# The second layer norm's mean by an extra projection column and its squares on ScalarE, in a hybrid attention kernel

## The chip, the cores and the metric

The kernel runs on one core of one Trainium2 chip. The metric is the device time of one execution in microseconds (us). The engines are called PE (TensorE), DVE (VectorE), ACT (ScalarE), POOL (GpSimd) and SP (SyncE); ACT, SP and POOL also issue DMA transfers, each from its own queue. L978 is line 978 of the kernel before; the lines of the kernel after are higher by one to thirty.

## The reference, cut to what matters

Input is an image of 256 channels and 64 x 64 pixels, in float32. Layer 0 is a windowed linear attention on group-normalised channels and is added to the image. Layer 1 takes the 4096 pixels as tokens of 256 channels:

```python
t = t + attention(layer_norm(t))          # 8 heads of 32, softmax over 4096 keys, w_out, b_out
t = t + experts(layer_norm(t))            # the second norm: of what the line above gave
# layer_norm: (v - mean(v)) / sqrt(var(v) + 1e-5), over the 256 channels of a token
# experts: norm once more, two of 8 experts for each token by softmax of xt @ Wr,
#          gelu(xe @ W1) @ W2, weighted sum
```

The change is about the second norm: each token's mean and variance over its channels after the attention's output has been added.

## The kernel before, in words

All activations stay in on-chip memory. The residual stream is the tile `t`, 32 token tiles of 128 tokens by 256 channels and 8 more columns: the tokens' scores for the 8 experts before normalisation. The weight `wo` (attention's output projection) has the same 8 more columns, made on PE from `w_out` and `Wr`, so one projection gives both a tile's attention output and its part of the scores.

The stages are layer 0 (to about 1037 us), the first norm and the projections to queries, keys and values (to 1155), the attention (1155 to 2412), routing (to some 2460), 36 expert slots, and the output.

The attention goes over eight chunks of 512 queries (`qc`), two groups of four heads (`g`), and 32 tiles of 128 keys (`i`). A step `i` is:
- PE: four products of keys and queries, one a head, into two pairs of banks of `ps_two` (L969; three pairs are there),
- ACT: two exponentials of 1024 columns into one buffer of `pe` (L978; four buffers),
- DVE: the buffer is added to `total`, for the denominators (L984), except at steps 0, 15 and 31 (step 1 adds the two first),
- PE, one step later: the products with the values, accumulated in `ps_acc` (L938), and at steps 15 and 31 also the products with ones, into the denominator bank `ps_den`, which has one buffer.

Work for the end of a group is spread over the next group's steps by a list of chains: `take` (copy of `ps_acc`, L1001), `pack` (the products of `total` with ones, the copy of `ps_den` to `rec`, L1022, and two transfers that pack the denominators densely), three empty steps, `turn` (the reciprocal, L1030, and five transfers that spread it again), three empty steps, `spread` (the multiplication, L1007).

When chunk `qc - 1` is done for both head groups, its four token tiles are projected. This is put into the steps of group `g = 1` of chunk `qc`:

```python
if qc and g == KC - 1 and i in range(5, NT // 2, 3):
    done.append(NB * (qc - 1) + len(done) % NB)
    project(den_bank(), done[-1])
```

so at steps 5, 8, 11 and 14, into the denominator bank that is not in use there. `project` is two matmuls (L919), an addition to `t` on DVE (L922) and `norm2.stats`, two DVE instructions (L740 and L741). The last four tiles are projected behind the loop.

The order of instructions on an engine isn't that of the code alone: a scheduler places each instruction when the kernel is built, by its own estimate of when its data are there. Engines then run their own instructions in that fixed order and wait for each other by semaphores.

Behind the attention, the second norm is finished (L745 to L749), the normalised tokens `z` are made by ACT (L1195) and stored, and the experts' scores are corrected by mean and deviation (L1209 to L1212). Small weights for the experts come by ACT's queue (L1172), are transposed by PE (L1174) and copied by DVE (L1175).

Of the kernel before, what the change touches and what calls it, by code (L numbers as in the profile page):

```python
# [34 lines left out]
NT = N // P  # L35
# [5 lines left out]
NB = IMG // BH  # L41
# [5 lines left out]
NE = 8  # L47
# [64 lines left out]
def tile_conv_attn_hybrid(ctx: ExitStack, tc: tile.TileContext, a: dict, out: bass.AP):  # L112
    nc = tc.nc

    const = ctx.enter_context(tc.tile_pool(name="const", bufs=1))
    keep = ctx.enter_context(tc.tile_pool(name="keep", bufs=1))
# [15 lines left out]

    t = keep.tile([P, NT, C + NE], F32, name="t")

    wr_sum = keep.tile([P, NE], F32, name="wr_sum")
    act = keep.tile([P, KC, N], F32, name="act")

    def tok(i):  # L140
        return slice(P * i, P * (i + 1))
# [44 lines left out]
    with ExitStack() as phase:  # L186
        wts = phase.enter_context(tc.tile_pool(name="c_wts", bufs=1))
# [22 lines left out]
        with (  # L210
# [34 lines left out]
            for b in range(NB):  # L245
# [6 lines left out]
                for ix in range(0, NCH, 2):  # L252
                    tp = bank("tp")
# [6 lines left out]
                    to, tp = tb[:, b, ix : ix + 2, :C], tp.rearrange("p (i c) -> p i c", c=C)  # L260
# [24 lines left out]
            rstd = rstd_of(small, var_ps[:, :KC], KC, 1e-5)  # L285
            for k in range(KC):
# [5 lines left out]
                    op0=ALU.subtract,  # L292
                    op1=ALU.mult,
# [461 lines left out]
            nc.tensor.transpose(tp[:, tok(k)], src[:, tok(k)], ident)  # L755
        nc.scalar.copy(dst, tp[:, :C].rearrange("p (k n) -> p k n", k=KC))

    norm2 = Norm(keep, "ln2")


    with ExitStack() as phase:
        pool = lambda name, bufs: phase.enter_context(tc.tile_pool(name=name, bufs=bufs))
        big = pool("a_big", 1)
        wts = pool("a_wts", 1)
        small = pool("a_small", 1)

        wo = wts.tile([P, KC, C + NE], F32, name="wo")
        nc.scalar.dma_start(wo[:, :, :C], a["L1_attn_w_out"].rearrange("(k p) o -> p k o", p=P))


# [6 lines left out]
        with (  # L777
# [23 lines left out]
            for n, by in enumerate((lambda k: ones[:, :1], lambda k: bqk[:, 4 + k : 5 + k])):  # L801
                for k in range(KC):
# [4 lines left out]
                        start=k == 0,  # L807
                        stop=k == KC - 1,
# [5 lines left out]
            for j in range(KC):  # L814
                tp = ps.tile([P, CH], F32, tag="mm", name="ps_mm")
# [3 lines left out]
            tp = ps.tile([P, CH], F32, tag="mm", name="ps_mm")  # L819
            for k in range(KC):  # L820
                for j in range(KC):
# [4 lines left out]
                        start=j == 0,  # L826
                        stop=j == KC - 1,
                    )
            nc.vector.tensor_copy(wo[:, :, C:], tp[:, : KC * NE].rearrange("p (k e) -> p k e", e=NE))

            norm = Norm(small, "ln1")

# [6 lines left out]
            for c in range(NCH):  # L839
                if c + 1 < NCH:  # L840
                    begin(c + 1)
                norm.end(NB * c, NB * (c + 1))
                for i in range(NB * c, NB * (c + 1)):
                    hn = work.tile([P, C], F32, name="hn")
                    nc.vector.tensor_scalar(
                        hn,
                        t[:, i, :C],
                        norm.mean[:, i : i + 1],
                        norm.rstd[:, i : i + 1],
                        op0=ALU.subtract,  # L850
                        op1=ALU.mult,
                    )
                    to_channels(hn, act[:, :, tok(i)], ps)

                    nc.gpsimd.tensor_add(t[:, i, :C], t[:, i, :C], bo)
                for s in range(2):
                    for g in range(KC):
                        m = KC * s + g
                        pr = ps.tile([P, CH], F32, tag="mm", name="ps_mm")
                        for k in range(KC):  # L860
                            nc.tensor.matmul(
                                pr, wqkv[:, k, tok(m)], act[:, k, chunk(c)], start=k == 0, stop=k == KC - 1
                            )
                        to = qk[:, s, g, chunk(c)]
                        nc.vector.tensor_scalar_add(to, pr, bqk[:, m : m + 1])
                        nc.vector.tensor_reduce(
                            peak[:, s, g, c : c + 1], to, AX.X, ALU.max, apply_absolute_value=True
                        )
                for i in range(NB * c, NB * (c + 1)):
                    pv = ps.tile([P, CH], F32, tag="mm", name="ps_mm")  # L870
                    for k in range(KC):
                        nc.tensor.matmul(
                            pv[:, : C + NE],
                            act[:, k, tok(i)],
                            wqkv[:, k, 2 * C :],
                            start=k == 0,
                            stop=k == KC - 1,
                        )
                    nc.vector.tensor_add(v[:, i, :], pv[:, :C], bv)
                    nc.scalar.copy(t[:, i, C:], pv[:, C : C + NE])  # L880


            on_experts = lambda z: z.unsqueeze(2).to_broadcast([P, NT, NE])
            on_tiles = lambda z: z.unsqueeze(1).to_broadcast([P, NT, NE])
            std = win.tile([P, NT], F32, name="std")
            nc.vector.tensor_scalar_add(std, norm.var, 1e-5)
            nc.vector.tensor_mul(std, std, norm.rstd)
            nc.vector.tensor_mul(t[:, :, C:], t[:, :, C:], on_experts(std))
            shift = win.tile([P, NT, NE], F32, name="shift")
            nc.vector.tensor_mul(shift, on_experts(norm.mean), on_tiles(wr_sum))  # L890
            nc.vector.tensor_add(shift, shift, on_tiles(bo_wr))
            nc.vector.tensor_add(t[:, :, C:], t[:, :, C:], shift)

# [11 lines left out]
            tp = ps.tile([P, CH], F32, tag="mm", name="ps_mm")  # L905
# [9 lines left out]
        attnT = act  # L915

        def project(pr, i):
            for k in range(KC):
                nc.tensor.matmul(  # L919
                    pr[:, : C + NE], attnT[:, k, tok(i)], wo[:, k, :], start=k == 0, stop=k == KC - 1  # L920
                )
            nc.vector.tensor_add(t[:, i, :], pr[:, : C + NE], t[:, i, :])  # L922
            norm2.stats(i)

        with tc.If(tame > 0) as branch:  # L925
            with (
# [5 lines left out]
                def two_banks():  # L932
                    return ps.tile([P, 2, CH], F32, tag="two", name="ps_two", bufs=3)
# [16 lines left out]
                by_ones = (NT // 2 - 1, NT - 1)  # L950
# [3 lines left out]
                done = []  # L954

                def den_bank():
                    return ps.tile([P, CH], F32, tag="den", name="ps_den")

                for qc in range(NCH):
                    for g in range(KC):  # L960
# [4 lines left out]
                        for i in range(NT):  # L965
                            sc = [two_banks() for _ in range(2)]
                            for hd in range(4):
# [5 lines left out]
                                    start=True,  # L973
                                    stop=True,
# [21 lines left out]
                            if i == NT - 1:  # L996
                                to = attnT[:, g, chunk(qc)]
# [41 lines left out]
                                def spread(times=times, held=held):  # L1039
                                    times(held.pop())  # L1040

                                wait = [lambda: None] * 3
                                if qc == NCH - 1 and g == KC - 1:
                                    stages = [take, divide]
                                else:
# [1 line left out]
                            behind(*stages)  # L1047


                            if qc and g == KC - 1 and i in range(5, NT // 2, 3):  # L1050
                                done.append(NB * (qc - 1) + len(done) % NB)
                                project(den_bank(), done[-1])
                flush()
                for i in range(len(done), NT):
                    project(two_banks()[:, 0, :], i)
        with branch.Else():


            with (
# [8 lines left out]
                for hd in range(2 * 4):  # L1068
                    g, hs = hd // 4, slice(D * (hd % 4), D * (hd % 4 + 1))
                    nc.vector.tensor_copy(ka[:D, :], qk[hs, 1, g, :])  # L1070
                    for qc in range(NCH):
# [16 lines left out]
                        for i in range(NT):  # L1088
# [4 lines left out]
                            for j, lhsT in enumerate((v[:, i, D * hd : D * (hd + 1)], ones)):  # L1093
# [4 lines left out]
                                    start=i == 0,  # L1098
# [5 lines left out]
                        nc.vector.tensor_mul(attnT[hs, g, chunk(qc)], acc[:D, :], rec)  # L1104
                for i in range(NT):
                    project(ps.tile([P, CH], F32, tag="sc", name="ps_sc"), i)

    with ExitStack() as phase:
# [17 lines left out]
        def one(name):  # L1129
            return small.tile([P, NT], F32, name=name)  # L1130
# [30 lines left out]
        with ExitStack() as routing:  # L1161
# [18 lines left out]

            norm = norm2
            norm.begin(0, NT)
            norm.end(0, NT)
            again = one("again")
            nc.vector.tensor_mul(again, norm.var, norm.rstd)
            nc.vector.tensor_mul(again, again, norm.rstd)
            again = rstd_of(small, again, NT, 1e-5)
            nc.vector.tensor_mul(again, again, norm.rstd)  # L1190
            less = one("less")
            nc.vector.scalar_tensor_tensor(less, norm.mean, -1.0, again, op0=ALU.mult, op1=ALU.mult)
            z = big.tile([P, NT, C], F32, name="z")
            for i in range(NT):
                nc.scalar.activation(  # L1195
                    z[:, i, :], t[:, i, :C], AF.Identity, scale=again[:, i : i + 1], bias=less[:, i : i + 1]
                )
# [11 lines left out]
            nc.vector.tensor_mul(logit, on_experts(norm.mean), on_tiles(wr_sum))  # L1209
            nc.vector.tensor_sub(logit, t[:, :, C:], logit)  # L1210
            nc.vector.tensor_mul(logit, logit, on_experts(norm.rstd))
            nc.vector.tensor_add(logit, logit, on_tiles(br))  # L1212

            rank = on_tiles(cst["rank"])
# [258 lines left out]
```

## Time and profile before

| | |
|---|---|
| three runs | 3022.8, 3024.1 and 3033.7 us, median 3024.1 |
| the profiled execution | 3024.6 us; its span, from first to last instruction, 3022.8 us |
| attention loop, PE / DVE / ACT busy (1158 to 2400, 1242 us) | 1196.4 / 1114.3 / 993.2 us |
| busy over the span: PE, DVE, ACT, POOL | 94%, 68%, 50%, 25% |
| mean granted clock of PE | 0.97 |
| DVE, L740: 64 statistics of 256 columns, mean | 417 ns |
| DVE, L741: 64 aggregations, mean | 174 ns |
| DVE, L922: 28 additions in the loop, mean | 425 ns |

The page gives groups of instructions: line, engine, operation, output and inputs, how many, then busy time in us and the mean of one in ns, then the engine's idle time just before them and what ended most of it. A line of waits gives the waiting instruction, the one it waited for, the total in us, how often, and the longest. A line of the timeline gives start, duration, engine, line and operation, how many in a row, and in brackets the idle time before it. A matmul's end is modelled, and four matmuls of 32 rows run beside each other, so their durations don't add up.

### The profile page before, as it was taken

Reading aid. Unit: us, or ns where it says so; the run is one execution under the profiler, and the core shown is the slowest. Engines: PE = TensorE matmul, PEld = TensorE weight load, DVE = VectorE, ACT = ScalarE, POOL = GpSimd, SP = SyncE. Lnnn points to the kernel's source line nnn. Section 1 sums busy time; section 2 is a strip of 40 time slices with the busy share of each in tenths; the row PEclk is TensorE's granted clock in tenths of the full one; section 3 lists DMA queues with packets and bytes.
Section 4 is the critical chain, followed back from the end, with each engine's and each line's share of the span. In section 5 each row is a group of like instructions: output and inputs, shape, how many; then the busy total and the mean of one; then the engine's idle time right before and its main releaser. Section 6 shows DMA issues by size and latency. Waiting matters only on the chain.

```text
span 3022.8 us, 62433 instructions
## 1 busy us (share of the span) xinstructions
PE 2835.8 (94%) x26550; PEld 1366.5 (45%) x26550; DVE 2067.7 (68%) x2510; ACT 1510.2 (50%) x2079; POOL 742.6 (25%) x832
## 2 busy tenths in 40 slices
PE   6899999989999899999999999999999879999996
PEld 5456443736543453222222222222222248888884
DVE  5776768577677787998888988898889841111113
ACT  2242323133233216887878787878778642222222
POOL 4085857128577420000000000000000012222220
PEclk9999999999999999999999999999999969999997
DMA  2000000000000000000000000000000055566565
GB/s 84 6 2 4 2 3 2 7 1 3 3 2 3 18 1 1 5 5 5 5 5 5 5 5 5 5 5 5 5 5 5 6 186 194 187 202 190 195 194 197
DMA packets 92627, 133.24 MB, mean 44 GB/s; under 512 B 16914, under 2 KB 73976, under 8 KB 92340
## 3 DMA queue, kind: packets, MB, share of 16 engines
q1 hardware_dynamic: 78008, 101.12, 10.2%
q0 software_dynamic: 6912, 18.88, 2.2%
q10 hardware_dynamic: 7420, 9.15, 0.9%
q8 instruction: 212, 3.47, 0.5%
q14 instruction: 75, 0.61, 0.1%
HBM read 111.00 MB, written 18.12 MB: 43 GB/s over the span
## 4 chain that ended last, share of the span: by engine, by line
PE 32%; DVE 23%; DMA 2%; ACT 2%; issue 1%; SPq 0%; DVEq 0%; POOL 0%; ACTq 0%; POOLq 0%
DVE total L984 22%; PE ps_yp L1394 8%; PE ps_hp L1387 8%; PE ps_two L969 7%; PE ps_acc L938 6%; PE ps_den L938 1%; ACT pe L978 1%; DMA y<-yrows 1%; PE ps_acc L1311 1%; ACT z L1195 1%; PE ps_tp L1362 1%; DMA rec<-recs 0%; DMA recs<-some 0%; DMA some<-dens 0%; DMA dens<-rec 0%
## 5 line engine op out<-in xcount | busy, mean ns | idle before, releaser
L978 ACT ACTIVATE pe<-ps_two 128x1024 f32<-128x1024 f32 x1024 | 992.9, 1022 | 246.9 <-PE ps_two L969 219.9
L984 DVE TENSOR_TENSOR total<-total,pe 128x2048 f32<-128x2048 f32 x448 | 1024.9, 2288 | 56.3 <-ACT pe L978 16.1
L969 PE MATMUL ps_two<-qk 32*128 32x512 f32 x4096 | 639.9, 644 | 3.6 <-POOLq L925 1.9
L938 PE MATMUL ps_acc<-pe,v 128*32 128x512 f32 x4096 | 551.4, 610 | 27.0 <-DVE act L1001 26.8
L533 ACT COPY sm<-ps_sc 128x384 f32<-128x384 f32 (+4 forms) x486 | 232.6, 513 | 462.9 <-PE ps_sc L657 272.7
L537 POOL TENSOR_TENSOR sm<-sm,mask 128x192 f32<-128x192 f32 (+3 forms) x460 | 380.2, 863 | 227.7 <-ACT sm L533 227.2
L969 PEld LDWEIGHTS ps_two<-qk 32*128 32x128 f32 x4096 | 211.1, 184 | 425.8 <-PE ps_two L969 250.7
L537 DVE TENSOR_TENSOR sm<-ps_sc,mask 128x384 f32<-128x384 f32 (+3 forms) x708 | 323.8, 518 | 91.0 <-PE ps_sc L657 89.9
L1388 ACT ACTIVATE hid<-ps_hp,cols 128x256 f32<-128x256 f32 x288 | 136.5, 474 | 382.3 <-PE ps_hp L1387 382.3
L1237 POOL MEMSET on<- 128x256 f32 x1 | 0.3, 312 | 1256.1 <-PE ps_den L938 1256.1
L938 PEld LDWEIGHTS ps_acc<-pe,v 128*32 128x32 f32 x4096 | 81.0, 108 | 420.7 <-issue 379.7
L1387 PE MATMUL ps_hp<-xe,w 128*128 128x256 f32 x1152 | 256.3, 381 | 0.0
L1394 PE MATMUL ps_yp<-w,hid 128*128 128x256 f32 x1152 | 254.6, 379 | 0.0
L657 PE MATMUL ps_sc<-qk 32*128 32x192 f32 (+3 forms) x2688 | 243.8, 444 | 4.6 <-DVE sm L537 2.9
L1394 PEld LDWEIGHTS ps_yp<-w,hid 128*128 128x128 f32 x1152 | 216.4, 190 | 28.1
L1387 PEld LDWEIGHTS ps_hp<-xe,w 128*128 128x128 f32 x1152 | 208.2, 190 | 41.9 <-ACT hid L1388 5.2
L673 PE MATMUL ps_acc<-sm,v 128*32 128x192 f32 (+3 forms) x2688 | 216.1, 422 | 0.8 <-POOL sm L537 0.8
L1366 DVE TENSOR_SCALAR xe<-ps_tp,cols 128x256 f32<-128x256 f32 x72 | 35.8, 540 | 248.5 <-PE ps_tp L1362 228.7
L537 POOL TENSOR_TENSOR sm<-sm,ycut 128x384 f32<-128x384 f32 (+4 forms) x150 | 150.9, 1026 | 145.6 <-ACT sm L533 145.4
L657 PEld LDWEIGHTS ps_sc<-qk 32*128 32x128 f32 x2688 | 125.8, 186 | 122.5 <-DVE sm L537 69.8
L537 DVE TENSOR_TENSOR sm<-ps_sc,ycut 128x512 f32<-128x512 f32 (+4 forms) x250 | 127.5, 562 | 71.6 <-PE ps_sc L588 69.7
L1396 DVE TENSOR_TENSOR y<-ps_yp,b 128x256 f32<-128x256 f32 x72 | 30.6, 425 | 208.1 <-PE ps_yp L1394 208.1
(235 smaller groups left out, 2303.9 us busy)
## 6 DMA issues: line engine op xcount, KB each, us to landing
w<-in_L_ffn_W SPq DMA_DIRECT2D x72, 1024.0 KB
b<-in_L_ffn_b SPq DMA_DIRECT2D x36, 128.0 KB
zrows<-z SPq DMA_DIRECT2D x4, 1024.0 KB
y<-yrows SPq DMA_DIRECT2D x8, 512.0 KB
y<-yrows ACTq DMA_DIRECT2D x8, 512.0 KB
rec<-recs SPq DMA_DIRECT2D x60, 64.0 KB
x<-in_x ACTq DMA_DIRECT2D x4, 512.0 KB
x<-in_x SPq DMA_DIRECT2D x4, 512.0 KB
```

The source lines that it names most:

```text
L533: nc.scalar.copy(sm[:, :used], sc[:, :used])
L537: engine.tensor_mul(to, of, mk.unsqueeze(1).to_broadcast(list(to.shape)))
L657: nc.tensor.matmul(scs[h][:, at : at + n], kT[hs[h], tok(i)], qT[hs[h], CH * ix + CELL * c0 : CH * ix + CELL * c1], start=True, stop=True, ...
L673: nc.tensor.matmul(acc[hs[h], CELL * c0 : CELL * c1], v[:, i, hs[h]], sms[h][:, at : at + n], start=not begun[0], stop=last and at == plac ...
L938: nc.tensor.matmul(to[D * hd : D * (hd + 1), :], lhsT(hd), rhs[:, hd, :], start=start, stop=stop, skip_group_check=True,)
L969: nc.tensor.matmul(sc[hd // 2][:, hd % 2, :], qk[hs, 1, g, tok(i)], qk[hs, 0, g, chunk(qc)], start=True, stop=True,)
L978: nc.scalar.activation(pe[:, 2 * pair : 2 * pair + 2, :], sc[pair], AF.Exp, scale=C**-0.5)
L984: nc.vector.tensor_add(total, first if i == 1 else total, pe)
L1366: nc.vector.tensor_scalar(xe[:, k, :], tp[:, k, :], cols[:, gain], cols[:, shift], op0=ALU.mult, op1=ALU.add,)
L1387: nc.tensor.matmul(hp, w1[:, k, tok(n)], x_now[:, k, :], start=k == 0, stop=k == KC - 1)
L1388: nc.scalar.activation(hid[:, n, :], hp, AF.Gelu, bias=cols[:, n : n + 1])
L1394: nc.tensor.matmul(yp, hid[:, n, tok(j)], w2[:, n, :], start=n == 0, stop=n == NH - 1)
```

## The change

- `t` and `wo` get one more column. The column of `wo` is minus the mean of its 256 output columns, made by a reduction and a multiplication on DVE when the weights are there; that of `t` starts as minus the first norm's mean and minus the mean of `b_out`. A projection then leaves minus the new token's mean in that column of `t`.
- `norm2.stats` goes. In its place `square(i)` has ACT compute the sum of squares of the tile's rows less their mean, by an activation with that column as bias and an accumulating output, into a column of `squares`.
- Projections are asked for at steps 2, 5, 8 and 11, the square of each at the next of these steps or at 15. The last four tiles have their squares behind their projections.
- The chains that end a group have four empty steps in place of three, twice.
- Variance, deviation and the corrections behind the attention are made from `squares` and the new column.

```diff
-    t = keep.tile([P, NT, C + NE], F32, name="t")
+    CX = C + NE + 1
+    t = keep.tile([P, NT, CX], F32, name="t")
...
+            def less_mean(to, rows):
+                nc.vector.tensor_reduce(to, rows, AX.X, ALU.add, negate=True)
+                nc.vector.tensor_scalar_mul(to, to, 1 / C)
+
+            less_mean(wo[:, :, C + NE], wo[:, :, :C])
+            bo_mean = win.tile([P, 1], F32, name="bo_mean")
+            less_mean(bo_mean, bo)
...
+            nc.vector.scalar_tensor_tensor(
+                t[:, :, C + NE], norm.mean, -1.0, bo_mean.to_broadcast([P, NT]), op0=ALU.mult, op1=ALU.add
+            )
...
         def project(pr, i):
             for k in range(KC):
-                nc.tensor.matmul(
-                    pr[:, : C + NE], attnT[:, k, tok(i)], wo[:, k, :], start=k == 0, stop=k == KC - 1
-                )
-            nc.vector.tensor_add(t[:, i, :], pr[:, : C + NE], t[:, i, :])
-            norm2.stats(i)
+                nc.tensor.matmul(pr[:, :CX], attnT[:, k, tok(i)], wo[:, k, :], start=k == 0, stop=k == KC - 1)
+            nc.vector.tensor_add(t[:, i, :], pr[:, :CX], t[:, i, :])
+
+        def square(i):
+            junk = small.tile([P, C], BF16, tag="junk", name="junk")
+            nc.scalar.activation(
+                junk, t[:, i, :C], AF.Square, bias=t[:, i, CX - 1 :], accum_out=squares[:, i : i + 1]
+            )
...
-                                wait = [lambda: None] * 3
+                                wait = [lambda: None] * 4
...
-                            if qc and g == KC - 1 and i in range(5, NT // 2, 3):
-                                done.append(NB * (qc - 1) + len(done) % NB)
-                                project(den_bank(), done[-1])
+                            if qc and g == KC - 1 and i in (2, 5, 8, 11, by_ones[0]):
+                                if i > 2:
+                                    square(done[-1])
+                                if i < by_ones[0]:
+                                    done.append(NB * (qc - 1) + len(done) % NB)
+                                    project(den_bank(), done[-1])
                 flush()
                 for i in range(len(done), NT):
                     project(two_banks()[:, 0, :], i)
+                    square(i)
...
-            norm = norm2
-            norm.begin(0, NT)
-            norm.end(0, NT)
+            less = t[:, :, CX - 1]
+            var = one("var")
+            nc.vector.tensor_scalar_mul(var, squares, 1 / C)
+            rstd = one("rstd2")
+            nc.vector.tensor_scalar_add(rstd, var, 1e-5)
+            nc.scalar.sqrt(rstd, rstd)
+            nc.vector.reciprocal(rstd, rstd)
```

More of the change, by code (lines that the diff above doesn't have):

```diff
@@ L756, in to_channels @@
         nc.scalar.copy(dst, tp[:, :C].rearrange("p (k n) -> p k n", k=KC))
-    norm2 = Norm(keep, "ln2")
+    squares = keep.tile([P, NT], F32, name="squares")
     with ExitStack() as phase:
@@ L765, in tile_conv_attn_hybrid @@
         small = pool("a_small", 1)
-        wo = wts.tile([P, KC, C + NE], F32, name="wo")
+        wo = wts.tile([P, KC, CX], F32, name="wo")
         nc.scalar.dma_start(wo[:, :, :C], a["L1_attn_w_out"].rearrange("(k p) o -> p k o", p=P))
@@ L828, in tile_conv_attn_hybrid @@
                     )
-            nc.vector.tensor_copy(wo[:, :, C:], tp[:, : KC * NE].rearrange("p (k e) -> p k e", e=NE))
+            nc.vector.tensor_copy(
+                wo[:, :, C : C + NE], tp[:, : KC * NE].rearrange("p (k e) -> p k e", e=NE)
+            )
[5 more added lines that the diff above has]
+            less_mean(bo_mean, bo)
             norm = Norm(small, "ln1")
@@ L879, in tile_conv_attn_hybrid @@
                     nc.vector.tensor_add(v[:, i, :], pv[:, :C], bv)
-                    nc.scalar.copy(t[:, i, C:], pv[:, C : C + NE])
+                    nc.scalar.copy(t[:, i, C : C + NE], pv[:, C : C + NE])
             on_experts = lambda z: z.unsqueeze(2).to_broadcast([P, NT, NE])
@@ L887, in tile_conv_attn_hybrid @@
             nc.vector.tensor_mul(std, std, norm.rstd)
-            nc.vector.tensor_mul(t[:, :, C:], t[:, :, C:], on_experts(std))
+            scores = t[:, :, C : C + NE]
+            nc.vector.tensor_mul(scores, scores, on_experts(std))
             shift = win.tile([P, NT, NE], F32, name="shift")
@@ L891, in tile_conv_attn_hybrid @@
             nc.vector.tensor_add(shift, shift, on_tiles(bo_wr))
-            nc.vector.tensor_add(t[:, :, C:], t[:, :, C:], shift)
+            nc.vector.tensor_add(scores, scores, shift)
+            nc.vector.scalar_tensor_tensor(
+                t[:, :, C + NE], norm.mean, -1.0, bo_mean.to_broadcast([P, NT]), op0=ALU.mult, op1=ALU.add
+            )
             top = small.tile([P, 2, KC], F32, name="top")
@@ L918, in project @@
             for k in range(KC):
-                nc.tensor.matmul(
-                    pr[:, : C + NE], attnT[:, k, tok(i)], wo[:, k, :], start=k == 0, stop=k == KC - 1
-                )
-            nc.vector.tensor_add(t[:, i, :], pr[:, : C + NE], t[:, i, :])
-            norm2.stats(i)
+                nc.tensor.matmul(pr[:, :CX], attnT[:, k, tok(i)], wo[:, k, :], start=k == 0, stop=k == KC - 1)
[4 more added lines that the diff above has]
+                junk, t[:, i, :C], AF.Square, bias=t[:, i, CX - 1 :], accum_out=squares[:, i : i + 1]
+            )
         with tc.If(tame > 0) as branch:
@@ L1106, in tile_conv_attn_hybrid @@
                     project(ps.tile([P, CH], F32, tag="sc", name="ps_sc"), i)
+                    square(i)
     with ExitStack() as phase:
@@ L1179, in tile_conv_attn_hybrid @@
             nc.scalar.dma_start(crows.rearrange("e p n -> p e n"), cols)
-            norm = norm2
-            norm.begin(0, NT)
-            norm.end(0, NT)
+            less = t[:, :, CX - 1]
[5 more added lines that the diff above has]
+            nc.vector.reciprocal(rstd, rstd)
             again = one("again")
-            nc.vector.tensor_mul(again, norm.var, norm.rstd)
-            nc.vector.tensor_mul(again, again, norm.rstd)
+            nc.vector.tensor_mul(again, var, rstd)
+            nc.vector.tensor_mul(again, again, rstd)
             again = rstd_of(small, again, NT, 1e-5)
-            nc.vector.tensor_mul(again, again, norm.rstd)
-            less = one("less")
-            nc.vector.scalar_tensor_tensor(less, norm.mean, -1.0, again, op0=ALU.mult, op1=ALU.mult)
+            nc.vector.tensor_mul(again, again, rstd)
+            shift = one("shift")
+            nc.vector.tensor_mul(shift, less, again)
             z = big.tile([P, NT, C], F32, name="z")
@@ L1195, in tile_conv_attn_hybrid @@
                 nc.scalar.activation(
-                    z[:, i, :], t[:, i, :C], AF.Identity, scale=again[:, i : i + 1], bias=less[:, i : i + 1]
+                    z[:, i, :], t[:, i, :C], AF.Identity, scale=again[:, i : i + 1], bias=shift[:, i : i + 1]
                 )
@@ L1208, in tile_conv_attn_hybrid @@
             logit = each("logit")
-            nc.vector.tensor_mul(logit, on_experts(norm.mean), on_tiles(wr_sum))
-            nc.vector.tensor_sub(logit, t[:, :, C:], logit)
-            nc.vector.tensor_mul(logit, logit, on_experts(norm.rstd))
+            nc.vector.tensor_mul(logit, on_experts(less), on_tiles(wr_sum))
+            nc.vector.tensor_add(logit, t[:, :, C : C + NE], logit)
+            nc.vector.tensor_mul(logit, logit, on_experts(rstd))
             nc.vector.tensor_add(logit, logit, on_tiles(br))
```

## The prediction

> **What bounds the kernel now.** I read the page's table of groups first, then the waits of the attention loop (1158 to 2400 us), then the timeline of single steps. All the change's repeated work lies in that loop: 16 groups of 32 key tiles, 8 query chunks times two groups of four heads, called g=0 and g=1.
>
> ```profile
> L978 ACT ACTIVATE pe<-ps_two 128x1024 f32<-128x1024 f32 x1024 | 992.9, 1022 | 246.9 <-PE ps_two L969 219.9
> L984 DVE TENSOR_TENSOR total<-total,pe 128x2048 f32<-128x2048 f32 x448 | 1024.9, 2288 | 56.3 <-ACT pe L978 16.1
> ```
> ```profile
> PE ps_acc L938 <- DVE act L1001: 26.8, 15, 2.6
> ...
> PE ps_den L938 <- DVE t L922: 16.6, 7, 2.5
> DVE some L1030 <- DMA some<-dens: 15.3, 14, 1.8
> DVE act L1007 <- DMA rec<-recs: 10.3, 15, 1.6
> ```
> A tile costs DVE one add (2.29 us, 2.40 from start to start), ACT two exponentials (4.01 us for two tiles below, so 2.0), PE some 2.17 (score and value products; the score starts two tiles apart, at 1568.26 and 1572.57, give 2.16). PE sets the pace; DVE is slower still, but skips two tiles in 32 (15 and 31) and may lag, since `pe` has four buffers. The two PE waits above are where the lag is paid: at each group's start, and in the seven g=1 groups with projections once more at tile 15, where the denominator bank is held until DVE has added the fourth projection:
>
> ```profile
> 1739.12 0.42 DVE L922 TENSOR_TENSOR t<-ps_den,t 128x264 f32<-128x264 f32 x1
> 1739.58 0.43 DVE L740 BATCH_NORM_STATS2 st<-t 128x6 f32<-128x256 f32 x1
> 1739.60 0.16 PEld L938 LDWEIGHTS ps_den<-pe,ones 128*32 128x32 f32 x8 [3.34 <-DVE t L922]
> 1739.60 1.06 PE L938 MATMUL ps_den<-pe,ones 128*32 128x512 f32 x8 [2.43 <-DVE t L922]
> ```
> The step after a projection shows what room ACT has:
>
> ```profile
> 1566.34 0.43 DVE L922 TENSOR_TENSOR t<-ps_den,t 128x264 f32<-128x264 f32 x1
> ...
> 1567.17 1.16 PE L919 MATMUL ps_den<-wo,act 128*128 128x264 f32 x4
> ...
> 1568.26 1.14 PE L969 MATMUL ps_two<-qk 32*128 32x512 f32 x8
> 1569.33 0.16 PEld L938 LDWEIGHTS ps_acc<-pe,v 128*32 128x32 f32 x8 [0.76 <-issue]
> 1569.33 1.07 PE L938 MATMUL ps_acc<-pe,v 128*32 128x512 f32 x8
> 1569.43 4.01 ACT L978 ACTIVATE pe<-ps_two 128x1024 f32<-128x1024 f32 x4 [1.22 <-PE ps_two L969]
> ```
> PE's projection takes 1.09 to the next score, ACT is idle 1.22, and starts 1.17 after that score's start. DVE adds *this* projection's result only at 1574.33 (the L922 above is that of the one before): 7.2 us after its matmul, because three adds stand ahead of it.
>
> [...] an engine's instruction waits for its semaphores; I take it that what is behind it waits too, as DVE does at L1030 and L1007 here. [...] after the 2.62 us stalls at group starts some of the windows of 3.41 us are at half speed (eight matmuls in 1.71 instead of 0.88), and once after one of 1.78.
>
> **The change, part by part.**
>
> *DVE's norm statistics leave the loop*: 28 times 0.43 + 0.18 = 17 us of DVE. PE sets the pace, so they count only through lag, which the chain below carries.
>
> *One more step for transfers.* In the compiled order of DVE and of SP's queue, L1022, L1030, L1007 and their 7 transfers stand where they stood, after the same number of adds (two, one, two). The instructions are placed by the scheduler, not at the step where the code asks for them. I count nothing; the DMA waits of g=0 stay. Bound from the two rows: a gain of up to 26 us of DVE idle, of which little is PE's.
>
> *Projections from the third tile.* On PE the first now stands right behind the denominator sum of the previous group (call the end of that sum W = 0) and two steps' matmuls. Its bank is that sum's, free only when DVE has copied it (L1022):
>
> ```profile
> 1696.53 0.68 DVE L1001 COPY act<-ps_acc 128x512 f32<-128x512 f32 x1
> ...
> 1700.87 2.29 DVE L984 TENSOR_TENSOR total<-pe 128x2048 f32<-128x2048 f32 x1 [3.65 <-PE ps_den L938]
> ...
> 1703.08 0.68 DVE L1022 COPY rec<-ps_den 128x512 f32<-128x512 f32 x1
> ```
> The sum ended at 1700.68, the copy at 1703.76: W+3.1. PE is there at W+2.1, so a new PE wait of 1.05. The stall at tile 15 goes: the fourth projection is now at tile 11, added long before.
>
> *Squares on ACT.* In the compiled order the four squares of a g=1 group are not at tiles 5, 8, 11, 15, but pulled up between the two exponentials of tiles 3, 6, 9, 12, the first tiles behind each projection. Each waits for DVE's add of that very projection, behind the add of tile 2, 5, 8, 11. (The squares' scratch tile has one buffer, but ACT alone writes it: no wait.) Queued behind the square on ACT is the second half of that tile's exponential, for which both DVE's next add and PE's next value product wait. So ACT, which could run up to four tiles ahead, must here wait for DVE, and DVE then for ACT.
>
> Worked for one g=1 group, in us from W, with the durations above:
> - Projection 1 at 3.15, done 4.24; add of tile 2 from 3.1 to 5.4, L922's successor done 5.75. First exponential of tile 3 ends at 6.45, the square is free to run: 0.5, second exponential ends at 8.0 (0.5 late).
> - DVE: add 3 at 8.1, add 4 at 10.45, L1007 to 13.35, add 5 to 15.7, projection add to 16.05. PE has made projection 2 at 12.35, ACT tile 6's first exponential at 14.55; it waits 1.5 for DVE, square, second exponential at 17.65.
> - From there a closed loop: three adds 0.1 + 3 times 2.395, projection add 0.34, signal 0.08, square 0.5, second exponential 1.0 = 9.2, where PE alone would need 3 times 2.17 + 1.09 = 7.6. Tile 9's exponential ends at 26.85, tile 12's at 36.05.
> - Tiles 12 to 15 at PE's pace: denominator matmuls of tile 15 at 43.7, tile 17's first exponential at 45.9.
>
> In the profile of before that exponential starts at W + 41.2, 41.9, 41.1, 41.4, 43.0, 42.6 and 41.0: mean 41.7. **+4.15 a group, times 7 = +29.0.** Behind tile 17 DVE is fresh in both kernels (it idles 1.34 there before), so the half group and the next start are as before.
>
> *Clock.* PE now idles 1.7 to 2.1 at three places of each such group, near the 1.78 that once halved the clock. A halved window costs up to 1.6 (the products of one tile and a half take twice their time); at 21 places between none and half: 0 to +17. I take **+6**, about four.
>
> *Setup.* Four more DVE instructions before the first chunk: a reduce of 512 (0.68 as L866), one of 256 (0.42), two small ones (0.15 each) = 1.4, partly in DVE's idle 2.29 before L796, but the first waits for the weight transfer. Nothing to +2.5; I take **+1.5**. The small operation at its end (0.2) is in this.
>
> *Tail.* The four last squares keep ACT in the branch until about 2411.9. Behind them on ACT's queue are the bias and three row loads (L148, L1172), which ACT issues at 2399.24 to 2412.49 now, and the table load for the root:
>
> ```profile
> 2412.85 1.28 ACT L746 ACT_TABLE_LOAD   x1 [14.76 <-PE ps_mm L1174]
> ...
> 2415.28 0.30 DVE L1175 COPY cols<-ps_mm 128x64 f32<-128x64 f32 x2 [0.25 <-issue]
> ```
> With 1 to 2.7 us for the branch (ACT's and DVE's gaps here), 1.5 of issue and some 2.5 to land, L1175 comes at 2416.8 to 2418.3, and the third load's copy, also in DVE's queue, near 2421. The statistics that DVE saves here (0.9) are covered by that. 0 to +5; **+3**.
>
> *The 265th column* adds 0.4% to 265-column operations: nothing; [...]
>
> Sum: 29.0 + 6 + 1.5 + 3 = 39.5 on the profiled execution's own 3024.6, which lies 0.5 above the median of 3024.1: **3064**.
>
> **Rivals.**
> - *Faster.* DVE is ahead whenever a square comes, ACT never waits, and what remains is the tile-15 stall gone: 7 times 2.43 = 17 and two half-speed windows behind it (3): 3004.6. The mechanism is DVE's lag; it decides in this direction if the projection's add ends before the first exponential of the next tile does. For: DVE loses 0.6 per projection. Against: three adds take 7.2, the projection's matmul comes late in them. 6%.
> - *Only the small costs.* Squares find their data, and cost their own 0.55 each, as ACT has only 0.17 a tile to spare: 4 times 0.55 + 1.05 - 2.43 = +0.8 a group, 6 in all; with setup and tail 3035. 9%.
> - *The clock takes over.* All 21 stalls halve it: 29 + 34 + 4.5 and longer squares (0.2 times 28 = 6): 3098. 9%.
> - *The extra step does act* and saves g=0's DMA waits: at most 8 groups times 1.7 (15.3 + 10.3 over 15 groups) = 14 off the first case: 3050, inside its range; against it stands the compiled order.
>
> **How the numbers follow.** The first case gets 76%, with 3048 to 3085. 0.5% (15 us) is about what a measurement of this kernel can tell from no change. Faster by more: the first rival, 6%; within: the second, 9%; slower 85%. The range leaves out the first rival and most of the third: 3034 to 3092.
>
> **What would show it.** Right: in the waits, ACT waiting for DVE's projection add some 1.5 us, 21 times; the second exponential of tiles 3, 6, 9, 12 detached from the first; adds at L984's successor idling 1.6 for ACT in the same places; the wait of PE for that add at tile 15 gone, one of 1 us before projection 1 instead; DMA waits as before. Wrong: squares running inside ACT's idle 1.2 without a wait, and tile 17 at W+42 or earlier.

## The result, and the profile after

| | before | after |
|---|---|---|
| median of five runs each | 3024.1 us | 3052.2 us (3049.3 to 3055.4) |
| ratio | | 1.0087, interval 1.0070 to 1.0103 |
| profiled execution; its span | 3024.6; 3022.8 | 3053.7; 3051.9 |
| layer 0 (to the start of its last addition to `t`) | 1037.4 | 1040.7 |
| setup (from there to the first score) | 118.3 | 120.1 |
| attention loop (first score to end of the last exponential) | 1242.4 | 1262.6 |
| tail (from there to the start of `z`) | 21.1 | 25.0 |
| loop's seven g=1 groups with projections, mean | 82.6 | 85.7 |

Slower by 28 us; the two profiled executions differ by 29. 20 of it is in the loop, 4 in the tail, 2 in the setup. The 3 in layer 0 can't be put down to the change: in both profiles the granted clock of PE was 0.50 in some stretches of layer 0 (41 us of them before, 55 after), partly at other places. Its last addition started at 1037.4 to 1043.8 in the four kernels without the extra column and at 1034.1 to 1044.0 in the six with it. So the runs below, one profile each, are compared by stage first, and by ratio to the kernel before on the same chip (3022.0 us on the chip of the first four, 3029.2 on that of the others). Two executions of the experiments had a much lower mean clock than all others: one of 3042.9 us at 0.94, counted in the ratio of the late squares, whose interval it widens, and one of 3541.7 us at 0.74, left out of that of the kernel without squares.

The page's two groups, answering to those of before (busy time and mean, then idle time ahead of them and what ended it):

```profile
L998 ACT ACTIVATE pe<-ps_two 128x1024 f32<-128x1024 f32 x1024 | 992.3, 1022 | 227.7 <-PE ps_two L989 206.1
L1004 DVE TENSOR_TENSOR total<-total,pe 128x2048 f32<-128x2048 f32 x448 | 1026.2, 2291 | 101.0 <-ACT pe L998 62.5
```

ACT's and DVE's main instructions of the loop have not become slower: 1022 and 2291 ns, where it was 1022 and 2288. What grew is DVE's idle time ahead of its adds, 56.3 before, and what ended it is ACT, 16.1 before. The waits between 1158 and 2440 us say who holds whom (total us, how often, longest):

```profile
DVE total L1004 <- ACT pe L998: 69.5, 48, 7.0
...
ACT junk L941 <- DVE t L937: 37.2, 24, 9.8
...
PE ps_acc L958 <- DVE act L1021: 25.3, 15, 2.6
...
PE ps_acc L958 <- ACT pe L998: 13.4, 21, 1.2
DVE some L1050 <- DMA some<-dens: 10.5, 12, 1.4
...
DVE act L1027 <- DMA rec<-recs: 6.1, 9, 1.7
PE ps_den L936 <- DVE rec L1042: 5.0, 6, 1.2
```

ACT's squares (`junk`) wait for DVE, DVE's adds wait for ACT, and 21 times (three in each of seven groups) PE's value products wait for ACT. The wait of PE for DVE's projection addition at tile 15 is gone; a new one, of 0.2 to 1.2 in six of the seven groups, stands ahead of projection 1. The timeline of one turn of this loop, at tile 9 of a g=1 group, PE's score products, weight loads and DMA issues left out:

```profile
1732.35 1.07 PE L958 MATMUL ps_acc<-pe,v 128*32 128x512 f32 x8
1732.54 1.03 ACT L998 ACTIVATE pe<-ps_two 128x1024 f32<-128x1024 f32 x1 [1.25 <-PE ps_two L989]
1734.12 0.42 DVE L937 TENSOR_TENSOR t<-ps_den,t 128x265 f32<-128x265 f32 x1
1734.64 0.51 ACT L941 ACTIVATE junk<-t 128x256 bf16<-128x256 f32 x1 [1.07 <-DVE t L937]
1734.67 1.05 PE L958 MATMUL ps_acc<-pe,v 128*32 128x512 f32 x4
1735.05 0.19 ACT L941 ACTIVATION_READ_ACCUMULATOR junk<-t 128x1 f32 x1
1735.14 2.83 ACT L998 ACTIVATE pe<-ps_two 128x1024 f32<-128x1024 f32 x3
1736.18 7.08 DVE L1004 TENSOR_TENSOR total<-total,pe 128x2048 f32<-128x2048 f32 x3 [1.64 <-ACT pe L998]
1736.20 1.05 PE L958 MATMUL ps_acc<-pe,v 128*32 128x512 f32 x4 [0.48 <-ACT pe L998]
```

ACT makes the first half of the tile's exponential, stands 1.07 until DVE has added the projection, squares, and only then makes the second half; DVE, which waited 1.64, starts the next of its three adds 1.04 after that half started. PE's eight value products of the tile are split in two: the first four take 1.05 alone, as long as eight together (1.07 in the first line, where the page has 0.607 as the mean of one), and behind them PE idles 0.48. These two make the 1.5 us by which a turn is longer than PE alone needs.

The loop's delay can be read at one place in each group. W is the end of the products of `total` with ones, as in the prediction; the first exponential of tile 17 started at W+41.0 to 43.0 before (mean 41.7) and at W+45.0 to 45.4 after (mean 45.2). This number is used for all runs.

### The profile page after: what moved, and what is told of

Same layout as the page of the kernel before. It is cut to its first block, busy times and chain, and to the rows that moved or that the text cites. A ratio compares the mean times of both kernels' runs of the same rounds, so it can differ in the third digit from the quotient of the medians.

```text
span 3051.9 us, 62496 instructions
## 1 busy us (share of the span) xinstructions
PE 2862.6 (94%) x26550; PEld 1375.1 (45%) x26550; DVE 2052.8 (67%) x2452; ACT 1525.9 (50%) x2143; POOL 738.4 (24%) x832
## 5 line engine op out<-in xcount | busy, mean ns | idle before, releaser
L998 ACT ACTIVATE pe<-ps_two 128x1024 f32<-128x1024 f32 x1024 | 992.3, 1022 | 227.7 <-PE ps_two L989 206.1
L1004 DVE TENSOR_TENSOR total<-total,pe 128x2048 f32<-128x2048 f32 x448 | 1026.2, 2291 | 101.0 <-ACT pe L998 62.5
L958 PE MATMUL ps_acc<-pe,v 128*32 128x512 f32 x4096 | 573.7, 607 | 38.8 <-DVE act L1021 25.3
L1397 DVE TENSOR_SCALAR xe<-ps_tp,cols 128x256 f32<-128x256 f32 x72 | 35.8, 540 | 248.8 <-PE ps_tp L1393 228.7
```

The lines of the kernel that those rows point to most:

```text
L958: nc.tensor.matmul(to[D * hd : D * (hd + 1), :], lhsT(hd), rhs[:, hd, :], start=start, stop=stop, skip_group_check=True,)
L998: nc.scalar.activation(pe[:, 2 * pair : 2 * pair + 2, :], sc[pair], AF.Exp, scale=C**-0.5)
L1004: nc.vector.tensor_add(total, first if i == 1 else total, pe)
L1397: nc.vector.tensor_scalar(xe[:, k, :], tp[:, k, :], cols[:, gain], cols[:, shift], op0=ALU.mult, op1=ALU.add,)
```

## The experiments

Theory: the cost is ACT's waiting, in order, for DVE's addition of the projection just made, with the exponential that DVE and PE need queued behind it. Rivals: ACT's own time for 28 squares; the early projections; and, in the other direction, the extra empty steps doing something. In the four kernels of the change that differ in the squares alone (as measured above, late, one instruction later, none in the loop), PE, DVE and ACT run the same 8668, 551 and 1025 other instructions of the loop in the same order.

**Late squares.** The squares stay on ACT, each fixed behind the exponential of the step where the code asks for it. In the trace they stand behind both exponentials of tiles 5, 8, 11 and 15, so ahead of those of the tiles 6, 9, 12 and 16 that the expectation names:

```diff
-                                nc.scalar.activation(
+                                last = nc.scalar.activation(
...
-                                    square(done[-1])
+                                    with tc.issue_after(last.ins):
+                                        square(done[-1])
```

> The changed kernel, with one dependency of order more: each square of a g=1 group is placed on ACT behind the exponential of the step at which the code asks for it, so at tiles 6, 9, 12 and 16, three tiles after its projection, in place of between the two exponentials of the first tile behind it. The same 28 squares, on the same engine; everything else is as in the changed kernel. If ACT's waiting for DVE's addition of the projection is the cost (the theory), no square waits now, three of four fall into ACT's idle 1.2 us beside the next projection, and the seven g=1 groups fall from 85.7 to about 81 to 82: 3015 to 3020 us, faster than the kernel before by the tile-15 stall (7 times 2.4) less the new wait before projection 1 (7 times 1.1) less setup (1.9) and tail (4.0). If the cost is ACT's own time for 28 squares (28 times 0.5 to 0.7 = 14 to 19 us, near the measured +20 of the loop), the place makes no difference: 3050. If it is the early projections themselves, also 3050.

Measured: ratio 0.9978 (0.9944 to 1.0011), so about a point faster than the changed kernel. Six of its seven executions took 3005.6 to 3011.5, each less than any of the kernel before on that chip (3015.3 to 3026.7). Loop 1223.4, tile 17 at W+39.6, and 80.0 for the mean of the seven groups, a little better than the 81 to 82 expected. The loop is 39.2 us shorter than after the change, and 7 times (45.2 - 39.6) is 39.2. Of the wait of 37.2 us in 24 places only the 9.8 at the tail are left:

```profile
ACT junk L941 <- DVE t L937: 9.8, 1, 9.8
...
PE ps_den L936 <- DVE rec L1042: 7.5, 7, 1.2
```

Its timeline shows a square beside the next projection, without a wait, and the next exponential held by its score alone:

```profile
1708.84 1.16 PE L936 MATMUL ps_den<-wo,act 128*128 128x265 f32 x4
1709.77 0.51 ACT L941 ACTIVATE junk<-t 128x256 bf16<-128x256 f32 x1
...
1710.17 0.20 ACT L941 ACTIVATION_READ_ACCUMULATOR junk<-t 128x1 f32 x1
...
1711.13 3.98 ACT L998 ACTIVATE pe<-ps_two 128x1024 f32<-128x1024 f32 x4 [0.76 <-PE ps_two L989]
```

The same instructions on the same engine, two and a half to three and a half tiles later: the rival of ACT's own time falls.

**No squares in the loop.**

```diff
+    nc.gpsimd.memset(squares, 1.0)
...
-                                if i > 2:
-                                    square(done[-1])
```

> The changed kernel without the 28 squares of the loop (the sums of squares of these tiles are left out: their column of `squares` stays at 1, set by POOL at the start; the four tiles behind the loop keep theirs). An upper bound of what squares cost. Theory and rivals: about 3013 to 3018 us. What tells them apart is how near the kernel with late squares comes to this one: within 4 us by the theory of the wait, 15 to 20 us above it if ACT's own time is the cost. If this one too stays near 3050, the squares are not the cause at all.

Measured: 0.9974 (0.9965 to 0.9983), loop 1226.7, tile 17 at W+39.5. Leaving the 28 squares out gives no more than placing them late. Well placed, they cost nothing that can be measured here. Everything else of the change in the loop (the 265th column, the early projections, the extra steps) is in this kernel too, so none of that is the cost. The two loops, 1223.4 and 1226.7, also show how far single profiles scatter: their seven groups take 80.0 us each in both.

**Early projections alone**, in the kernel before:

```diff
-                            if qc and g == KC - 1 and i in range(5, NT // 2, 3):
+                            if qc and g == KC - 1 and i in range(2, 12, 3):
```

> The kernel before with its projections asked for at steps 2, 5, 8, 11 in place of 5, 8, 11, 14; norm statistics stay on DVE, no square on ACT. By the theory the early projections are a gain: the stall of 2.43 at tile 15 goes in seven groups, the wait for the copy of the denominators before projection 1 costs 1.1: net 7 times -1.3 = -9, and a clock window or two: 3010 to 3016 us. If instead the early projections are what made the changed kernel slower (the bank not free, DVE behind in its first tiles), this one is slower than before: 3030 to 3045.

Measured: 0.9964 (0.9952 to 0.9976), loop 1222.8, tile 17 at W+39.5. This part of the change is a gain on its own, of 2.2 us a group against before (41.7 - 39.5): more than the 1.3 expected, in part because in three of the seven groups of before tile 17 came another 0.7 to 1.8 us behind the mean of the other four (41.2), and here in none. The new wait before projection 1 is 7.5 us in 7 groups.

**One more empty step alone**, in the kernel before:

```diff
-                                wait = [lambda: None] * 3
+                                wait = [lambda: None] * 4
```

> The kernel before with four empty steps in place of three in the chains that end a group, and nothing else. The instructions stand in the same order on every engine as before. Theory: 3024 us, no difference, and the waits of DVE for `some` and `rec` as they were (15 and 10 us). If the extra step acted, those waits would shrink and it would give up to 14 us: 3010.

Measured: 1.0005 (0.9992 to 1.0018), loop 1242.8 against 1242.4, and the waits of DVE for the transfers as before:

```profile
DVE some L1030 <- DMA some<-dens: 14.1, 14, 1.9
DVE act L1007 <- DMA rec<-recs: 10.6, 15, 1.5
```

The extra step does nothing that shows. The changed kernel's smaller waits there (10.5 and 6.1) are not its doing: the kernel with early projections alone, with three empty steps and no square, has 9.0 and 6.6.

**Squares one instruction later**, behind the second exponential of the same tile in place of ahead of it:

```diff
-                            if qc and g == KC - 1 and i in (2, 5, 8, 11, by_ones[0]):
-                                if i > 2:
-                                    square(done[-1])
-                                if i < by_ones[0]:
-                                    done.append(NB * (qc - 1) + len(done) % NB)
-                                    project(den_bank(), done[-1])
+                            if qc and g == KC - 1 and i in (3, 6, 9, 12):
+                                with tc.issue_after(last.ins):
+                                    square(done[-1])
+                            if qc and g == KC - 1 and i in (2, 5, 8, 11):
+                                done.append(NB * (qc - 1) + len(done) % NB)
+                                project(den_bank(), done[-1])
```

> The changed kernel with each square one instruction later on ACT: behind the second exponential of tiles 3, 6, 9, 12 in place of ahead of it. ACT still waits there for DVE's addition of the same projection, but what DVE needs for its next add is no longer queued behind it. Theory of the loop (ACT waits for DVE, then DVE for ACT): call the end of the projection's addition X; DVE adds tile 6 from X to X+2.4, the square ends at X+0.8, tile 7's two exponentials at X+2.8, so DVE idles only some 0.5 and the cycle of three tiles is about 8.05 us in place of 9.06 (PE alone needs 7.6). Tile 17's exponential at W+41.5 (changed kernel 45.2, late squares 39.6), so 3015 to 3024 us. If what costs is that ACT waits at all, whatever is behind it, it stays at 3045 to 3050. If only the place between two halves mattered and no loop remained, it equals the late squares: 3010.

Measured: 0.9989 (0.9982 to 0.9996), loop 1239.0, tile 17 at W+41.3, against 41.5 expected. Its timeline, at the same place of the group:

```profile
1725.08 1.16 PE L936 MATMUL ps_den<-wo,act 128*128 128x265 f32 x4
...
1727.43 1.94 ACT L998 ACTIVATE pe<-ps_two 128x1024 f32<-128x1024 f32 x2 [1.72 <-PE ps_two L989]
...
1728.52 0.43 DVE L937 TENSOR_TENSOR t<-ps_den,t 128x265 f32<-128x265 f32 x1
1729.26 0.51 ACT L941 ACTIVATE junk<-t 128x256 bf16<-128x256 f32 x1
1729.40 7.09 DVE L1004 TENSOR_TENSOR total<-total,pe 128x2048 f32<-128x2048 f32 x3 [0.45 <-ACT pe L998]
...
1732.88 1.16 PE L936 MATMUL ps_den<-wo,act 128*128 128x265 f32 x4
```

Both halves of the exponential are made in one piece (1.94), DVE idles 0.45 in place of 1.64, and PE's projections are 7.80 apart here, 8.07 the turn before (1717.01 to 1725.08), against 9.07 with the square between the halves (1730.18 to 1739.25) and 7.5 with late squares (1701.29, 1708.84, 1716.33). One place in ACT's order is worth 24 of the 39 us of the loop; the remaining 15 are what the next two to three tiles' delay brings, with no wait of a square left.

**The ends taken back**, with the loop as in the changed kernel:

```diff
-            less_mean(wo[:, :, C + NE], wo[:, :, :C])
             bo_mean = win.tile([P, 1], F32, name="bo_mean")
-            less_mean(bo_mean, bo)
...
+                        if c == 2 and m == 2 * KC - 1:
+                            with tc.issue_after(added.ins):
+                                less_mean(wo[:, :, C + NE], wo[:, :, :C])
+                                less_mean(bo_mean, bo)
...
-                nc.scalar.dma_start(rw, a[name].rearrange("e (k p) -> (e k) p", p=P))
+                nc.sync.dma_start(rw, a[name].rearrange("e (k p) -> (e k) p", p=P))
```

> The changed kernel with its two ends taken back and the loop as it is: the two means are made by DVE during the third chunk of the projections, no longer ahead of the first, and the three row loads for the experts are issued by SP's queue in place of ACT's, where they stand behind the last squares. Read by stage: from layer 0's last addition to the first score 120.1 should fall to 118.2 (before: 118.25), and from the last exponential to the first expert's products 68.7 to 65 or 66 (before: 64.7). If the tail's cost is the squares themselves or the new chain of small operations, the tail stays at 68 to 69. The loop stays at 1262.

Measured, in a single execution (3050.3 us): setup 118.5, loop 1263.4, first expert's products 65.3 behind the last exponential in place of 68.7 (`z` 21.8 in place of 25.0). The tail comes back by the queue of three transfers. After the change, ACT issues the loads behind its last square, and DVE waits for the transposed rows:

```profile
2440.83 0.60 ACTq L1199 DMA_DIRECT2D L_ffn_ln_g_rows<-in_L_ffn_ln_g  x1
...
2443.04 0.39 DVE L1202 COPY cols<-ps_mm 128x64 f32<-128x64 f32 x2 [3.36 <-PE ps_mm L1201]
```

With SP's queue the same load is issued at 2432.89, and DVE doesn't wait:

```profile
2439.87 0.31 DVE L1204 COPY cols<-ps_mm 128x64 f32<-128x64 f32 x2
```

`z` starts at 21.8 and 21.5 in the two kernels with these loads on SP's queue, at 23.2 to 26.1 in the four with them behind the squares. (With statistics on DVE it is 19.7 to 23.2 in four kernels, so a single profile is good to some 2 us.) The setup is less clear. With the means made early it was 120.1, 119.5, 118.6 and 118.6 in four kernels, and from 117.5 to 118.6 in the six others: about 0.9 on average, near the scatter.

**Projections one step later**, alone and with all the rest:

```diff
-                            if qc and g == KC - 1 and i in range(5, NT // 2, 3):
+                            if qc and g == KC - 1 and i in range(3, 13, 3):
```

> The kernel before with projections asked for at steps 3, 6, 9 and 12, and nothing else: norm statistics stay on DVE. Theory: both waits for the denominator bank go, that at tile 15 (2.4) and that before projection 1 (1.1 in the kernel with steps 2 to 11): 3010.6 less 7 times 1.1 = 3003 (2999 to 3006). Then moving the statistics to ACT is worth less than 5 us even at its best. Rival: DVE's statistics matter once the stalls are gone (17 us of DVE), and it stays at 3010 or above while the kernel with squares at their best reaches 2998.

The other kernel has the ends of the run above, and in the loop:

```diff
+                            if qc and g == KC - 1 and i in (6, 9, 12, 15):
+                                with tc.issue_after(last.ins):
+                                    square(done[-1])
+                            if qc and g == KC - 1 and i in (3, 6, 9, 12):
+                                done.append(NB * (qc - 1) + len(done) % NB)
+                                project(den_bank(), done[-1])
```

> The changed kernel with late squares, both ends taken back as in the run of the ends, and the projections asked for at steps 3, 6, 9 and 12, squares three steps later. One step later the denominator bank has been copied when projection 1 comes (copy ended at W+3.1, PE there at W+4.3), so its wait of 1.1 goes; the fourth projection's addition is still over before tile 15's denominator products. Theory: late squares' 3010 less 7 times 1.1 for the wait, less 1.9 and some 3 for the ends: 2998 (2994 to 3003). Rival: the later projection meets DVE's lag (its addition now stands between L1007's reciprocal and multiplication), nothing is won: 3004 to 3008.

Measured, on the same chip, where the kernel before took 3029.2: statistics on DVE 0.9955 (0.9943 to 0.9967), 3015.0, loop 1223.6; squares on ACT and all the rest 0.9924 (0.9908 to 0.9939), 3005.2, loop 1219.1. On the 3024.1 of the first runs these ratios would be 3010.5 and 3001. The second beats both kernels, and by ratio lies within its 2994 to 3003. The first missed its 3003: tile 17 did come a microsecond sooner than with steps 2 to 11 (W+38.5 against 39.5), but the loop didn't. Its waits beside those of the kernel with squares, first with statistics on DVE:

```profile
PE ps_acc L938 <- DVE act L1001: 32.9, 15, 2.6
...
DVE total L984 <- ACT pe L978: 9.3, 5, 7.0
```

and then with squares on ACT:

```profile
PE ps_acc L960 <- DVE act L1023: 25.3, 15, 2.6
...
DVE total L1006 <- ACT pe L1000: 22.1, 19, 7.0
```

With the statistics, DVE finds time to wait for ACT at 5 places in place of 19: it has not made up its lag when the second half of the group starts, ends the group later, and PE pays 7.6 us more at the starts of the next groups. 7.0 of these are at the starts that follow a g=1 group (13.5 against 6.6). So here, with the stalls ahead of it gone, taking the statistics from DVE is worth something: 4.5 us of loop in this pair of profiles. The rival of that expectation was right in its direction. (Of the other 5 us between the two kernels, layer 0 has 3 and the tail 2, both within what single profiles scatter.)

## Why the prediction was right

Forecast 3064 (+39.5), range 3034 to 3092, slower at 85%; measured 3052 (+28). The mechanism was right, the size of two of its terms was not. By its steps:

- **ACT waits for DVE's projection addition, and DVE for ACT**: shown. Moving the squares removes all of the loop's loss, moving them by one instruction removes the part worked out for it. The closed loop was put at 9.2 us and was 9.06. Sum of the step: 4.15 a group predicted, 45.2 - 41.7 = 3.5 measured, so 24 in place of 29. The chain was already 0.4 short at tile 12 (its second exponential ended at W+35.5 to 35.8, not 36.05) and 0.7 at tile 15 (W+43.0 in the mean, not 43.7). ACT waited the 1.5 expected at the first of the three places of a group (1.8 in one group) and 1.1 at the other two. The square was taken as 0.5, the author's estimate, near the 0.474 and 0.585 that other activations of 128x256 took on ACT in the profile before (L1388, L1195); it took 0.51 and delayed the second exponential by 0.50 (1734.64 to 1735.14). No table load stands between squares and exponentials: the only ACT_TABLE_LOAD of the loop after is at 1162.19 (1.28 us), ahead of its first exponential.
- **The first square runs without a wait**: so it was in six of the seven groups, where it started at once behind the first exponential of tile 3; in one it waited 0.25.
- **A new wait of 1.05 before projection 1, the stall at tile 15 gone**: 1.16 in the group of the timeline above, but 5.0 us in six groups together, where 7.4 were expected in seven; no wait at tile 15 in any.
- **Clock, +6**: this term failed. That some of these stalls would halve the clock was the author's estimate, with 1.7 to 2.1 of idle PE at each place. PE idles 0.5 to 0.9 in one piece (once 1.2), because four of a tile's eight value products need only the first exponential and run during the wait (the two halves of four at 1734.67 and 1736.20 above). Behind the first group's start, the loop after has seven half-speed windows (granted clock 0.50 for 3.41 us each), none at such a place, all at the starts of groups. Before had eight, two of them at the tile-15 stall: the one behind 1.78 us that the prediction names, and one at 1584.3, behind a stall of 2.53, that it overlooked. Behind the stall of 2.43 that ended at 1739.60 the clock stayed at 1.00. So the term came to nothing or slightly less, and why a window was halved behind some stalls of 2 us and more and not behind others stays open.
- **DVE's 17 us of statistics only by lag; nothing for the extra step**: the second is shown. The first held for this change; the last two runs show that the lag does have a price once the stalls are gone.
- **DMA waits as before**: wrong in size. They shrank from 15.3 and 10.3 to 10.5 and 6.1. The squares are not needed for it: early projections alone have 9.0 and 6.6, the kernel without squares in the loop 14.1 and 6.6. The cause stays open, and so does what it is worth.
- **Setup +1.5, tail +3**: 1.9 and 3.9 in the two profiles. In the tail, 2.5 us for a transfer to land was the author's estimate: PE's first products that waited for the rows issued at 2440.83 and 2443.04 started 1.8 and 1.6 later. That most of the tail is the row loads behind ACT's last squares is shown; that all of 1.9 is the early means is not. (By its own terms the copy L1175 would come at 2416.9 to 2418.6, not 2416.8 to 2418.3, which changes nothing.)

The loop is +20.2, and the seven groups with squares +22.3, of the 24 at their tile 17: what the prediction left as it was behind tile 17 gave back 2. The other nine groups gained 2.1, 1.6 of it in the first, which has a half-speed window in the profile before and none after. Loop, setup and tail make 26, layer 0 the other 3. The prediction did not have these 3, and as far as the runs tell they are chance; in this pair of profiles they bring the sum nearer to it.

## What to carry to other kernels

A small instruction put on an engine with idle time can cost what it makes others wait for, not what it takes: look at which instruction it stands ahead of in that engine's compiled order, and whether its input is made by an engine that lags. Where the code asks for it says little when a scheduler places it; fix its place behind something that is surely later than its input. And price the parts of a change apart: here the early projections gave 0.4%, and the place of 28 small instructions took 1.3% (39 us of loop).

## What the runs showed that I had not expected

Each of the 32 squares (ACTIVATE with an accumulating output, mean 0.507 us in the profile after) was followed by a second instruction of its own, ACTIVATION_READ_ACCUMULATOR, of 0.18 to 0.20 us. It cost less than it shows: in the turn above it started at 1735.05, while the square ran to 1735.15, and the next exponential started 0.09 after it, at 1735.14.
